# A peer-expert stage on one core: the residual on GpSimd, differences of p with six products, and the ones of c in bfloat16 from SBUF

## The chip, the core and the metric

The kernel runs on one core of a Trainium2 chip. The metric is device time in microseconds (us), the median over the runs shown; a profile is one execution with the hardware profiler on. The core has five engines with a queue of instructions each: TensorE (PE; its weight loads are shown as PEld), VectorE (DVE), ScalarE (ACT), GpSimd (POOL) and SyncE (SP), which here issues the transfers. An engine works through its queue in order and waits at an instruction until what it reads is written and what it writes over has been read.

## The reference

The inputs are 16 sequences of 512 tokens with 128 features. An attention with a window (16 heads, a token sees the 128 tokens before and after it) is added to x; then comes a layer with 1024 small experts, whose result is added too:

```python
s, i = jax.lax.top_k(sim, k)                      # per head: 8 best of 32 keys, twice
all_scores = (sx[..., :, None] + sy[..., None, :]).reshape(b, n, h, k * k)
all_idx = (ix[..., :, None] * nk + iy[..., None, :]).reshape(b, n, h, k * k)
scores, pk = jax.lax.top_k(all_scores, k)         # the 8 best of 64 sums
idx = jnp.take_along_axis(all_idx, pk, axis=-1)
w_down = key_in[idx]
w_up = key_out[idx]
o = jnp.einsum('bnd,bnhkd->bnhk', inputs, w_down)
o = jax.nn.gelu(o, approximate=False) * jax.nn.softmax(scores, axis=-1)
return jnp.einsum('bnhk,bnhkd->bnd', o, w_up)
```

So each token picks 8 heads times 8 = 64 experts (by number), with a share each.

## The kernel before

Two stages follow each other. The first is the attention, with the normalisations; the change leaves it alone. It ends with x after attention in SBUF (`xs[b]`) and its normalised transpose in DRAM.

The second stage, the experts, gathers nothing: all 1024 experts are computed for every token, and the picked ones are weighted. The number of an expert is written as p * 16 + c, with 64 values of p (`NP`) and 16 of c (`NC`). It works through 64 tiles of 128 tokens, i = 0 to 63; tile i is quarter t = i % 4 of sequence b = i // 4. For one tile:

1. DVE finds the best keys (`best_keys`, `where_keys`), the best sums and their places (`best_sums`, `where_sums`), POOL and DVE make the expert numbers from them (`pick_words` on POOL: two `word` instructions; then `numbers` on DVE, whose first instruction, `x_ps<-word,x_ps`, needs the second word). Below, t and "tile" mean this loop.
2. `turn`: ACT casts the numbers to bfloat16 (`num_bf`), PE transposes them into a PSUM bank (`turned`, in the profile `x_ps`) so that the 64 picks lie on the partitions, and 64 tokens of each half of the tile along the row. `turned[:, 0]` holds p times 16 and `turned[:, 1]` holds c. ACT copies the p part to `p_bf`.
3. Indicators ("ones") are made: of c on DVE (`ones_of_c`, tile `mine`: is c of this pick equal to 0..15?), multiplied on POOL with the pick's share (`weights_at_c`, four instructions, tile `cols`); of p for one half of the tokens on DVE (`ones_of_p`, two `row` instructions), for the other half through differences: PE puts p minus each number 0..63 into PSUM (`offs_of_p`, `off_ps`: four banks, two products each), ACT squares them (`off_p`) and takes Relu(1 - square) (`other_ones_of_p`, `row`).
4. `weigh`: for each token PE multiplies the indicators of p with the weighted indicators of c, which gives the tile's weight for every expert (`w_ps`); 128 small matmuls a tile in two halves, `m` = 0 and 1. ACT copies them out (`take_weights`, tile `g`), POOL multiplies by the gelu of the experts' inner products (`weigh_experts`, `g<-g,gel`).
5. PE multiplies with the experts' output rows (`up`, for an earlier sequence, a quarter at a time), and `finish` transposes a finished sequence (`o_ps`); `store` adds the residual and sends it off.

Beside it run the inner products of the next sequence (`down` on PE, `dn_ps`; `gelu` on ACT) and the scores of the tile after next (`score`, `take_scores`).

Every engine's order is written out by hand in the loop: whatever goes through `pe`, `dve`, `act`, `pool` keeps program order. What sets the order around the change, in one turn of the loop for tile i: `best_sums(i)`, the weights of half 0 of tile i-1, `where_sums`, `pick_words`, `numbers(i)`, `weigh(i-1, 1)` and half a quarter of `up` (`seconds`), `turn(i)`, `share_of(i)` and `sums_of_keys(i+1)` on POOL, the weights of half 1 of tile i-1, `where_keys(i+1)`, `offs_of_p(i)`, `turn_shares(i)` (`s_ps`), the ones of c and p, the other half of `seconds`, `down`, `score(i+2)` (`sim_ps`), the gelu, at t = 1 `scale` (`xb`) for the next sequence, and then, at t = 1, `finish` and `store` of sequence b-2, and `weigh(i, 0)`.

The PSUM pool `ps_x` has three buffers, used in turn by `off_ps`, `dn_ps`, `sim_ps` and `o_ps`. Lines 168, 172 and 615 of the profile are helpers that record operations, so one line stands for many; the tiles' names tell them apart. L330 is the normalisation on DVE, L368 and L369 are memsets in the attention stage: L369 writes one of every 32 numbers of a row (`va[:, :, :, DK : DK + 1]`).

Of the kernel before, what the change touches and what calls it, by code (L numbers as in the profile page):

```python
# [10 lines left out]
F32 = mybir.dt.float32  # L11
BF16 = mybir.dt.bfloat16
# [4 lines left out]
ALU = mybir.AluOpType  # L17
# [3 lines left out]
P = 128  # L21
# [6 lines left out]
def bc(ap, axis, n):  # L28

    ap = ap.unsqueeze(axis)  # L30
    shape = list(ap.shape)
    shape[axis] = n
    return ap.to_broadcast(shape)
# [10 lines left out]
def kernel(  # L44
# [13 lines left out]
    nc = tc.nc  # L58
    B, T, D = x.shape
    NH = 16  # L60
    DK = D // NH
    NQ = T // P
# [8 lines left out]
    const = ctx.enter_context(tc.tile_pool(name="const", bufs=1))  # L71
# [8 lines left out]
    xs = []  # L80
    for b in range(B):
        t = keep.tile([P, NQ, D], F32, name=f"x_{b}")
# [8 lines left out]
    NP, NC = P // 2, NE // (P // 2)  # L91
# [3 lines left out]
    ident = const.tile([P, P], F32, name="ident")  # L95
    make_identity(nc, ident)
    ident_bf = const.tile([P, P], BF16, name="ident_bf")
# [18 lines left out]
    def counted(shape, pattern, dtype, name, base=0):  # L116

        t_i = const.tile([P] + shape, I32, name=f"{name}_i")
        nc.gpsimd.iota(t_i, pattern=pattern, base=base, channel_multiplier=0)
        if dtype == I32:  # L120
            return t_i
        t = const.tile([P] + shape, dtype, name=name)
        nc.vector.tensor_copy(t, t_i)
        return t
# [2 lines left out]

    nums_p = counted([NP], [[NC, NP]], F32, "nums_p")
    nums_c = counted([NC], [[1, NC]], F32, "nums_c")
    less_nums = const.tile([P, NP], BF16, name="less_nums")  # L130
    nc.vector.tensor_scalar_mul(less_nums, nums_p, -1.0)

# [17 lines left out]
    out_v = out.rearrange("b (t p) d -> b p t d", p=P)  # L150


    with ExitStack() as at:
# [385 lines left out]
        for s in range(-2 * NG * NQ, (NU + 1) * NQ):  # L539
            n, u = divmod(s, NQ)  # L540
            b, g = divmod(n, NG)
# [53 lines left out]
    b2 = ctx.enter_context(tc.tile_pool(name="b2", bufs=2))  # L595
# [3 lines left out]
    ps_x = ctx.enter_context(tc.tile_pool(name="ps_x", bufs=3, space=PSUM))  # L599
    ps_t = ctx.enter_context(tc.tile_pool(name="ps_t", bufs=1, space=PSUM))  # L600
    HK = H * TOPK
    HT, QT = P // 2, P // 4
    NM = QT // 2
    HM = NM // 2
    halves = [slice(v * HT, v * HT + HT) for v in range(2)]
# [11 lines left out]
    pe, dve, act, pool = (InOrder(e) for e in (nc.tensor, nc.vector, nc.scalar, nc.gpsimd))  # L617
# [9 lines left out]
    xbs, downs, gels, gs, ups, outs_T = {}, {}, {}, {}, {}, {}  # L627
    sims, tops, cands, idxs, bytes_of, steps_of = {}, {}, {}, {}, {}, {}
    bests, ws, shares, places, shifts, words, nums, turned = {}, {}, {}, {}, {}, {}, {}, {}
    mines, rows, weights = {}, {}, {}  # L630
    p_bfs, wTs, offs = {}, {}, {}

    def scale(b):
        xb = b2.tile([P, T], F32, tag="xb", name=f"xb_{b}")
# [67 lines left out]
    def best_sums(j):  # L702
        best = b2.tile([P, H, TOPK], F32, tag="best", name=f"best_{j}")
        for h in range(H):
            dve.max(best[:, h], cands[j][:, h].rearrange("p a b -> p (a b)"))
        bests[j] = best
# [55 lines left out]
    def turn(j):  # L762

        num = b2.tile([P, 3, HK], BF16, tag="num_bf", name=f"num_bf_{j}")
        act.copy(num, nums.pop(j))
        for i, (to, what) in enumerate(((0, num[:, 0]), (0, num[:, 1]), (1, num[:, 2]))):
            for v in range(2):
                pe.matmul(
                    turned[j][halves[v], to], lhsT=what, rhs=ident_bf[:, halves[v]],
                    start=i == 0, stop=i != 0, skip_group_check=True,  # L770
                )
        p_bfs[j] = b2.tile([P, HT], BF16, tag="p_bf", name=f"p_bf_{j}")
        act.copy(p_bfs[j], turned[j][:, 0])

    def turn_shares(j):
        share = shares.pop(j).rearrange("p h k -> p (h k)")
# [9 lines left out]
    def take_shares(j):  # L786
        wT = b2.tile([P, HT], F32, tag="wT", name=f"wT_{j}")
        act.copy(wT, wTs[j])
        wTs[j] = wT

    def some(t, m, rows_of=slice(0, P)):

        return t.rearrange("p (v m n) -> p m v n", v=2, m=2)[rows_of, m]

    def ones_of_c(j):
        mine = b2.tile([P, 2, 2, NM, NC], BF16, tag="mine", name=f"mine_{j}")
        dve.tensor_tensor(
            mine.rearrange("p v m n c -> p (v m n) c"), bc(turned[j][:, 1], 2, NC),
            bc(nums_c, 1, HT), ALU.is_equal,
        )  # L800
        mines[j] = mine

    def weights_at_c(j, m):
        for s in range(2):
# [5 lines left out]
    def ones_of_p(j, m):  # L810
# [3 lines left out]
            ALU.is_equal,  # L814
        )

    def offs_of_p(j):

        for m in range(2):
            for n in range(0, NM, HM):  # L820
                off_ps = ps_x.tile([P, HM, NP], F32, tag="x", name=f"off_ps_{j}_{m}_{n}")
                for start, rhs in (
                    (True, bc(some(p_bfs[j], m)[:, 1, n : n + HM], 2, NP)),
                    (False, bc(less_nums, 1, HM)),
                ):
                    pe.matmul(off_ps, lhsT=ident_bf, rhs=rhs, start=start, stop=not start)
                off_p = b2.tile([P, HM, NP], BF16, tag="off_p", name=f"off_p_{j}_{m}_{n}", bufs=4)
                act.activation(off_p, off_ps, AF.Square)
                offs[j, m, n] = off_p
# [21 lines left out]
    def take_weights(j, m):  # L851
        b, t = divmod(j, NQ)
        if t == m == 0:
            gs[b] = b2.tile([P, NC, NQ, 2, QT], F32, tag="g", name=f"g_{b}")
        g = gs[b][:, :, t, :, m * NM : m * NM + NM]
        act.copy(g, weights.pop((j, m)).rearrange("p n (s c) -> p c s n", s=2))

    def weigh_experts(j, m):

        b, t = divmod(j, NQ)  # L860
        g = gs[b][:, :, t, :, m * NM : m * NM + NM]
        pool.tensor_tensor(g, g, gels[b][:, :, t, :, m * NM : m * NM + NM], ALU.mult)
# [17 lines left out]
    def finish(b):  # L880

        oT = outs_T.pop(b)
        o_ps = ps_x.tile([P, NQ, D], F32, tag="x", name=f"o_ps_{b}")
        for t in range(NQ):
            pe.transpose(
                o_ps[:, t], oT[:, 2 * t : 2 * t + 2].rearrange("d s v n -> d (s v n)"), ident
            )
        outs_T[b] = o_ps

    def store(b):  # L890
        o_sb = b2.tile([P, NQ, D], F32, tag="o_sb", name=f"o_sb_{b}")
        dve.tensor_add(o_sb, outs_T.pop(b), xs[b])
        nc.sync.dma_start(out_v[b], o_sb)


# [3 lines left out]
    NB = B * NQ  # L899

    def seconds(i, place):

        b, t = divmod(i, NQ)
        if b + 1 == B and t in (1, 2):
            up(b - 1, range(8 * t - 8 + 4 * place, 8 * t - 4 + 4 * place))
        elif i + 1 == NB:
            if place:
                up(b, range(NC), slice(0, NQ // 2))
        else:
            of, quarter = (b - 1, t - 1) if t else (b - 2, NQ - 1)  # L910
            if of >= 0:
                c = 4 * quarter + 2 * place
                up(of, range(c, c + 2))
# [19 lines left out]
    for i in range(NB):  # L933
        b, t = divmod(i, NQ)
        before, behind = i > 0, i + 1 < NB
        best_sums(i)
        less_greatest(i)
        if before:
            take_weights(i - 1, 0)
        step_of_words(i)  # L940
        where_sums(i)
        pick_words(i)
        if before:
            weigh_experts(i - 1, 0)
        tops_of = best_keys(i + 1) if behind else iter(())
        next(tops_of, None)
        numbers(i)
        if before:
            weigh(i - 1, 1)
        seconds(i, 0)  # L950
        turn(i)
        for _ in tops_of:
            pass
        share_of(i)
        if behind:
            sums_of_keys(i + 1)
        if before:
            take_weights(i - 1, 1)
            weigh_experts(i - 1, 1)
        if behind:  # L960
            where_keys(i + 1)
        offs_of_p(i)
        turn_shares(i)
        take_shares(i)
        if behind:
            pack_keys(i + 1)
        for m in range(2):
            rows[i, m] = b2.tile([P, 2, NM, NP], F32, tag="row", name=f"row_{i}_{m}")
        ones_of_c(i)
        weights_at_c(i, 0)  # L970
        ones_of_p(i, 0)
        ones_of_p(i, 1)
        weights_at_c(i, 1)
        other_ones_of_p(i, 0)
        other_ones_of_p(i, 1)
        seconds(i, 1)
        if b + 1 < B:
            down(b + 1, 2 * t)
            down(b + 1, 2 * t + 1)
        if i + 2 < NB:  # L980
            score(i + 2)
            take_scores(i + 2)
        if b + 1 < B:
            gelu(b + 1, 2 * t)
            gelu(b + 1, 2 * t + 1)
        if t == 1:
            if b + 1 < B:
                scale(b + 1)
            if b + 2 < B:
                load(b + 2)  # L990
        ready = b - 2 if t == 1 else b - 1 if i + 1 == NB else -1
        if ready >= 0:
            finish(ready)
            store(ready)
        weigh(i, 0)
    take_weights(NB - 1, 0)
    weigh_experts(NB - 1, 0)
# [42 lines left out]
```

## Time and profile before

| what | us |
|---|---|
| three runs: median (lowest, highest) | 1604.19 (1594.6, 1605.45) |
| the profiled execution, its own time | 1607.73 |
| its span, first to last instruction | 1606.0 |
| first and last `best` of the experts' stage, start | 771.7, 1574.8 |

| engine | busy us in the span | share |
|---|---|---|
| PE | 1438.7 | 90% |
| DVE | 1359.5 | 85% |
| ACT | 1208.8 | 75% |
| POOL | 1078.4 | 67% |

The mean granted TensorE clock was 0.976 of full speed. The table's shares are over both stages, and the stages differ: a question about the experts has to be put to the rows of that stage.

A row of the timeline is read as: start and length in us, engine, line, operation, what is written <- what is read with sizes, how many merged, and in brackets how long the engine had stood idle before it and whose end released it. In a row of the instruction groups the numbers behind the bar are busy us, mean ns of one, and idle us before them.

### The profile page before, as it was taken

How to read it: one execution, taken by the hardware profiler on the slowest of the kernel's cores; microseconds unless marked ns; L12 is line 12 of the kernel's file. 1: busy time of each engine (PE TensorE's matmuls, PEld its weight loads, DVE VectorE, ACT ScalarE, POOL GpSimd, SP SyncE). 2: the span in 40 equal slices, each digit the busy share in tenths (PEclk: the TensorE clock that was granted, in tenths of full speed). 3: DMA queues.
4: the chain of work that ended last, by engine and by line, in shares of the span. 5: the costliest groups of instructions: out<-in, count | busy, mean ns of one | idle time of the engine just before them, and what ended most of it. 6: DMA issues, size and time to landing. Idle time of an engine off the chain costs nothing.

```text
span 1606.0 us, 49399 instructions
## 1 busy us (share of the span) xinstructions
PE 1438.7 (90%) x16880; PEld 844.4 (53%) x16880; DVE 1359.5 (85%) x8012; ACT 1208.8 (75%) x2579; POOL 1078.4 (67%) x1692
## 2 busy tenths in 40 slices
PE   4899999999999999986789999999999999999998
PEld 1344454444444444433456666666666666666666
DVE  6788778778878888885799999999999999999994
ACT  1477667667767777676698888888898888988863
POOL 7466666666667666545477777777777777777774
PEclk9899999999999999999799999999999999999998
DMA  6233322222223223221000000000000000000000
GB/s 180 66 103 95 95 76 81 79 70 80 71 71 94 86 81 96 82 61 53 9 9 10 9 15 9 15 16 9 15 9 15 16 9 16 9 16 9 9 9 14
DMA packets 53579, 75.00 MB, mean 47 GB/s; under 512 B 5840, under 2 KB 39888, under 8 KB 53200
## 3 DMA queue, kind: packets, MB, share of 16 engines
q1 hardware_dynamic: 52496, 71.59, 15.2%
q8 instruction: 133, 2.18, 0.6%
q14 instruction: 118, 0.97, 0.2%
q10 hardware_dynamic: 832, 0.26, 0.1%
HBM read 49.28 MB, written 20.97 MB: 44 GB/s over the span
## 4 chain that ended last, share of the span: by engine, by line
PE 36%; DVE 35%; ACT 10%; DMA 9%; POOL 6%; issue 3%; SPq 2%; DVEq 0%; POOLq 0%; ACTq 0%
PE o_ps L168 7%; PE s_ps L168 7%; DVE idx L615 7%; DVE row L615 6%; PE e_ps L168 5%; DMA qst<-qv 5%; DVE place L615 4%; DVE top L615 4%; DMA qst<-mT 4%; DVE best L615 3%; DVE mine L615 3%; PE off_ps L615 3%; PE dn_ps L615 3%; ACT L615 2%; DVE masked L415 2%
## 5 line engine op out<-in xcount | busy, mean ns | idle before, releaser
L415 DVE CUSTOM_DVE_ANT_0 masked<-s_ps,band 128x384 bf16<-128x384 f32 (+1 forms) x1024 | 498.3, 487 | 142.6 <-PE s_ps L168 40.4
L457 ACT ACTIVATE pT<-e_ps 128x384 f32<-128x384 f32 (+1 forms) x1024 | 390.6, 436 | 173.1 <-PE e_ps L168 165.2
L172 POOL TENSOR_SCALAR_AFFINE_SELECT pT<-pT 128x512 f32<-128x512 f32 x384 | 238.8, 638 | 238.9 <-ACT pT L457 238.8
L168 PE MATMUL s_ps<-kst,qst 128*128 128x384 bf16 (+1 forms) x1024 | 314.1, 308 | 45.9 <-DVE mx L415 14.9
L615 POOL TENSOR_TENSOR cols<-mine,wT 64x512 f32<-64x512 bf16 x256 | 269.8, 1054 | 51.8 <-DVE mine L615 29.1
L615 PEld LDWEIGHTS w_ps<-cols,row 128*64 128x64 f32 x8192 | 250.2, 139 | 48.4 <-POOL cols L615 42.8
L615 PE MATMUL w_ps<-cols,row 128*64 128x32 f32 x8192 | 259.4, 224 | 6.8 <-POOL cols L615 6.8
L168 PE MATMUL e_ps<-qst,kst 128*128 128x384 bf16 (+1 forms) x1024 | 226.8, 303 | 11.5 <-DMA qst<-mT 7.3
L615 POOL TENSOR_TENSOR g<-g,gel 128x512 f32<-128x512 f32 x128 | 163.6, 1278 | 87.9 <-ACT g L615 87.9
L168 PEld LDWEIGHTS <-qst 128*128 128x128 bf16 x1024 | 100.4, 98 | 217.6 <-issue 159.0
L168 PE MATMUL o_ps<-pT,vaug 128*32 128x384 f32 (+1 forms) x2048 | 192.8, 448 | 0.4 <-POOL pT L172 0.4
L615 DVE FIND_INDEX8 idx<-top,sim 128x8 uint32<-128x32 f32 x1024 | 166.2, 184 | 0.0
L615 ACT ACTIVATE row<-off_p,one 128x512 f32<-128x512 bf16 x256 | 165.7, 748 | 0.0
L615 ACT ACT_TABLE_LOAD x122 | 156.5, 1283 | 2.1
L615 DVE TENSOR_TENSOR row<-x_ps,nums_p 128x1024 f32<-128x1024 f32 x128 | 150.0, 1212 | 0.0
L615 PE MATMUL up_ps<-g,key_out_sb 64*128 64x256 f32 (+2 forms) x1152 | 148.1, 384 | 0.0
L615 ACT ACTIVATE off_p<-off_ps 128x512 bf16<-128x512 f32 x256 | 133.4, 601 | 19.4 <-PE off_ps L615 19.2
L615 PE MATMUL dn_ps<-xt,key_inT 128*64 128x256 f32 x1024 | 128.8, 396 | 0.0
L168 PEld LDWEIGHTS <-kst 128*128 128x128 bf16 x1024 | 98.1, 99 | 53.0 <-issue 19.2
L615 PE MATMUL off_ps<-p_bf,ident_bf 128*128 128x512 bf16 x256 | 99.1, 387 | 19.5 <-ACT p_bf L615 19.5
L615 DVE MAX8 top<-sim 128x8 f32<-128x32 f32 x1024 | 106.7, 177 | 5.5 <-ACT sim L615 5.5
L615 PEld LDWEIGHTS up_ps<-g,key_out_sb 64*128 64x128 f32 x1152 | 95.3, 189 | 12.4
(143 smaller groups left out, 2326.0 us busy)
## 6 DMA issues: line engine op xcount, KB each, us to landing
qst<-qv SPq DMA_DIRECT2D x192, 96.0 KB
kst<-kv SPq DMA_DIRECT2D x192, 96.0 KB
qv<-qp SPq DMA_DIRECT2D x16, 384.0 KB
kv<-kp SPq DMA_DIRECT2D x16, 384.0 KB
x<-in_L_attn_x_dram SPq DMA_DIRECT2D x16, 256.0 KB
xT<-xiT SPq DMA_DIRECT2D x16, 256.0 KB
xt<-xT SPq DMA_DIRECT2D x16, 256.0 KB
out_dram<-o_sb SPq DMA_DIRECT2D x16, 256.0 KB
```

Of the source, the lines that this page charges most:

```text
L168: tc.keep_in_program_order(nc.tensor.matmul(*args, **kw))
L172: tc.keep_in_program_order(getattr(nc.gpsimd, op)(*args, **kw))
L415: nc.vector.tensor_tensor_reduce(masked[:, 0:w], s, band.rearrange("p u k -> p (u k)")[:, from_u : from_u + w], 1.0, LOWEST, ALU.add, ALU. ...
L457: nc.scalar.activation(pT[:, h, 0:w], e_ps[:, 0:w], AF.Exp)
L615: return lambda *args, **kw: tc.keep_in_program_order(op(*args, **kw))
```

## The change

Three things are changed in the experts' stage, and two constants are added for them.

- The residual: at t = 1 ACT copies the transposed result from PSUM (`take_outs`), and in the next tile, t = 2, POOL adds x and the store is issued (`add_and_store`), between `take_weights(i - 1, 1)` and `weigh_experts(i - 1, 1)`. The last two sequences still use `store` on DVE.
- The differences of p: minus the numbers is put into two PSUM banks by two products before `turn` (`less_of_p`); then p of half m = 0 is added to them, ACT squares, and the difference between p of half 1 and p of half 0 is added to the same banks, and ACT squares again. For that the transposition uses `steps_bf` in place of the identity for p, so that the last 16 columns are differences. `p_bf` becomes 96 columns wide: the second half of p, and c.
- The ones of c: `mine` is compared from `p_bf` and a table `each_c` of all 16 values in 64 columns, both bfloat16 in SBUF; `mine` lies as (c, tokens) and is handed to `weights_at_c`, which is unchanged, as a view with c innermost.

```diff
+    steps_bf = const.tile([P, 2, P // 2], BF16, name="steps_bf")
+    nc.vector.tensor_copy(steps_bf.rearrange("p s n -> p (s n)"), ident)
+    for s in range(2):
+        nc.vector.tensor_sub(
+            steps_bf[:, s, 48:64], ident[:, 64 * s + 48 : 64 * s + 64],
+            ident[:, 64 * s + 32 : 64 * s + 48],
+        )
+    each_c = const.tile([P, NC, P // 2], BF16, name="each_c")
+    nc.vector.tensor_copy(each_c, bc(nums_c, 2, P // 2))
...
-                    turned[j][halves[v], to], lhsT=what, rhs=ident_bf[:, halves[v]],
+                    turned[j][halves[v], to], lhsT=what,
+                    rhs=ident_bf[:, halves[v]] if to else steps_bf[:, v],
...
-        p_bfs[j] = b2.tile([P, HT], BF16, tag="p_bf", name=f"p_bf_{j}")
-        act.copy(p_bfs[j], turned[j][:, 0])
+        p_bfs[j] = b2.tile([P, QT + HT], BF16, tag="p_bf", name=f"p_bf_{j}")
+        act.copy(p_bfs[j], turned[j].rearrange("p i n -> p (i n)")[:, QT : QT + QT + HT])
...
-        mine = b2.tile([P, 2, 2, NM, NC], BF16, tag="mine", name=f"mine_{j}")
-        dve.tensor_tensor(
-            mine.rearrange("p v m n c -> p (v m n) c"), bc(turned[j][:, 1], 2, NC),
-            bc(nums_c, 1, HT), ALU.is_equal,
-        )
-        mines[j] = mine
+        mine = b2.tile([P, NC, HT], BF16, tag="mine", name=f"mine_{j}")
+        dve.tensor_tensor(mine, bc(p_bfs[j][:, QT : QT + HT], 1, NC), each_c, ALU.is_equal)
+        mines[j] = mine.rearrange("p c (v m n) -> p v m n c", v=2, m=2)
...
+    def less_of_p(j):
+        diffs[j] = [ps_x.tile([P, HM, NP], F32, tag="x", name=f"off_ps_{j}_{i}") for i in range(2)]
+        for off_ps in diffs[j]:
+            pe.matmul(
+                off_ps, lhsT=ident_bf, rhs=bc(less_nums, 1, HM), start=True, stop=False,
+                skip_group_check=True,
+            )
...
-                off_ps = ps_x.tile([P, HM, NP], F32, tag="x", name=f"off_ps_{j}_{m}_{n}")
-                for start, rhs in (
-                    (True, bc(some(p_bfs[j], m)[:, 1, n : n + HM], 2, NP)),
-                    (False, bc(less_nums, 1, HM)),
-                ):
-                    pe.matmul(off_ps, lhsT=ident_bf, rhs=rhs, start=start, stop=not start)
+                off_ps = diffs[j][n // HM]
+                tokens = bc(p_bfs[j][:, m * NM + n : m * NM + n + HM], 2, NP)
+                pe.matmul(
+                    off_ps, lhsT=ident_bf, rhs=tokens, start=False, stop=True,
+                    skip_group_check=True,
+                )
...
+    def take_outs(b):
+        o_sb = b2.tile([P, NQ, D], F32, tag="o_sb", name=f"o_sb_{b}")
+        act.copy(o_sb, outs_T[b])
+        outs_T[b] = o_sb
+
+    def add_and_store(b):
+        o_sb = outs_T.pop(b)
+        pool.tensor_tensor(o_sb, o_sb, xs[b], ALU.add)
+        nc.sync.dma_start(out_v[b], o_sb)
...
         seconds(i, 0)
+        less_of_p(i)
         turn(i)
...
             take_weights(i - 1, 1)
+            if t == 2 and b >= 2:
+                add_and_store(b - 2)
             weigh_experts(i - 1, 1)
...
-        ready = b - 2 if t == 1 else b - 1 if i + 1 == NB else -1
-        if ready >= 0:
-            finish(ready)
-            store(ready)
+        if t == 1 and b >= 2:
+            finish(b - 2)
+            take_outs(b - 2)
+        if i + 1 == NB:
+            finish(b - 1)
+            store(b - 1)
         weigh(i, 0)
```

## The prediction

> **What bounds the kernel now.** I read the busy time by stretch first. The experts' stage runs from about 770 us to the end, 64 token tiles, and in its middle each 100 us looks like this (span, then busy time of PE, its weight loads, DVE, ACT, POOL; clock; DMA share; GB/s):
>
> ```profile
> 1100.00:1200.00 100.00, 91.99 (x1445) 62.27 (x1442) 94.12 (x675) 87.35 (x163) 73.58 (x96) 1.00 0.05 13
> ```
>
> Three engines are near full, POOL has a quarter free, the clock is full. So shares decide nothing, and I followed one group of four tiles (one sequence b, t = 0 to 3) in the timeline, engine by engine. ACT, columns start, length, instruction, idle before it:
>
> ```profile
> 1205.15 0.59 ACT L615 COPY sim<-sim_ps 128x512 f32<-128x512 f32 x1 [0.73 <-PE sim_ps L615]
> ...
> 1212.02 0.35 ACT L615 CAST num_bf<-num 128x192 bf16<-128x192 uint32 x1 [1.14 <-DVE num L615]
> ...
> 1231.38 0.59 ACT L615 COPY sim<-sim_ps 128x512 f32<-128x512 f32 x1 [0.73 <-PE sim_ps L615]
> ...
> 1236.31 0.35 ACT L615 CAST num_bf<-num 128x192 bf16<-128x192 uint32 x1
> ...
> 1243.53 0.59 ACT L615 COPY sim<-sim_ps 128x512 f32<-128x512 f32 x1 [0.26 <-PE sim_ps L615]
> ```
>
> PE and DVE in the same stretch:
>
> ```profile
> 1236.71 0.28 PE L615 MATMUL x_ps<-ident_bf,num_bf 128*64 128x64 bf16 x6 [0.35 <-ACT num_bf L615]
> ...
> 1239.16 0.34 PE L615 MATMUL s_ps<-ident,share 128*64 128x64 f32 x4
> ...
> 1242.37 1.13 PE L615 MATMUL sim_ps<-wsim,xb 128*128 128x512 f32 x2
> ```
>
> ```profile
> 1206.49 0.69 DVE L615 TENSOR_TENSOR o_sb<-o_ps,x 128x512 f32<-128x512 f32 x1 [2.39 <-PE o_ps L615]
> ...
> 1234.91 0.29 DVE L615 TENSOR_TENSOR x_ps<-word,x_ps 128x128 uint32<-128x128 uint32 x1
> ...
> 1239.29 1.20 DVE L615 TENSOR_TENSOR mine<-x_ps,nums_c 128x1024 bf16<-128x1024 f32 x1
> ```
>
> The reader is to see a ring through ACT and PE: ACT goes from sim to num_bf in 1236.31 + 0.35 - 1231.38 = 5.28 us, PE from x_ps to the end of sim_ps in 1243.50 - 1236.71 = 6.79, and with the hand-overs that is 12.15 us, sim to sim. DVE alone would need 11.87 a tile (it starts 1218.93, 1230.80, 1242.67) and catches up only because it is held once in four tiles: 2.39 us for o_ps plus 0.69 for the residual. The group takes 50.5 us (o_sb 1206.49 to 1257.01): three tiles near 12.15 and one of 14.
>
> POOL has its own ring, which is nearly as long:
>
> ```profile
> 1233.27 0.29 POOL L615 TENSOR_TENSOR w<-best 128x64 f32<-128x64 f32 x1
> ...
> 1234.45 0.43 POOL L615 TENSOR_TENSOR word<-word,packed 128x128 int32<-128x128 int32 x1
> 1236.49 1.28 POOL L615 TENSOR_TENSOR g<-g,gel 128x512 f32<-128x512 f32 x1 [1.61 <-ACT g L615]
> ...
> 1239.00 1.28 POOL L615 TENSOR_TENSOR g<-g,gel 128x512 f32<-128x512 f32 x1
> 1240.64 4.42 POOL L615 TENSOR_TENSOR cols<-mine,wT 64x512 f32<-64x512 bf16 x4 [0.36 <-DVE mine L615]
> ```
>
> Call T the end of the second word (1234.88). DVE's x_ps (numbers) starts 0.03 later, mine at T+4.41, the four cols at T+5.76 to T+10.18, and w, step, word, word need 1.41 (w's start 0.08 after cols): T' = T+11.7. So POOL's idle time is only inside the ring's DVE part; any lateness of cols over about 0.5 us becomes the tile's period.
>
> **The change, part by part.**
>
> *Residual.* DVE loses 0.69 + 2.39 us once in four tiles. But behind it ACT is next: sim at 1205.15, table load, two gel, xb 0.81, table load, w, g: num_bf could have started at 1210.88 (1212.02 less its idle 1.14). ACT now also copies o_ps (like the g copy, 0.59), so num_bf starts near 1211.45: gain 0.55 us of the 3.1 seen on DVE. POOL gets 128x512 f32 add once in four tiles, 1.28 by the g row, ahead of the second g and of cols. The store's DMA only moves half a tile later; nothing on SP waits for it.
>
> *Six products.* PE drops two of eight off_ps products at 0.215 (start to start). But two move ahead of x_ps, and PE waits there only 0.35 (and not at all in tile t = 3), so up to 0.4 comes on the ring. The third and fourth now write a bank that ACT's Square still reads: p_bf product, Square (0.60), product, Square. From 1237.30 (off_ps's first start) on: first Square 1237.74 (after ACT's g copy) to 1238.34, third product 1238.38, second Square to 1238.83, fourth product 1238.87, next matmul 1239.09 against 1239.16. So nothing is gained on PE; p_bf's 96 instead of 64 columns costs 0.03. Net 0 to +0.4 us a tile.
>
> *Ones of c on DVE.* mine is 1.20 us for 1024 outputs, or 1.12 start to start. No two-input bf16 operation from SBUF is in this trace, so: at worst 1.20 as now; by the Trainium skill (VectorE: DVE Perf Modes, the perf-mode tier table) tensor_tensor in dense bf16 from SBUF goes at twice the rate, so 512 of its 1024 cycles, 0.53 us at 0.96 GHz, go: 0.67. I take 0.67. On the ACT-PE ring it is worth nothing; on POOL's ring it brings cols forward 0.53.
>
> *Ones of c on POOL.* The new mine lies as (c, token); cols still reads c innermost, so each of its 512 elements now comes from 128 bytes further (64 bf16) instead of the next address. No POOL read of this kind is in the trace. The nearest rows are a 128-byte-stride write and a 16-byte-stride read of 16 elements:
>
> ```profile
> L615 POOL TENSOR_TENSOR step<-packed 128x16 int32<-128x16 int32 x64 | 15.0, 234 | 0.0
> ...
> L368 POOL MEMSET vaug<- 128x2048 f32 x3 | 5.4, 1815 | 0.0
> L615 POOL MEMSET cols<- 128x1024 f32 x2 | 1.8, 952 | 6.5 <-DVE bn_a L586 6.5
> L369 POOL MEMSET vaug<- 128x64 f32 x3 | 0.6, 209 | 0.0
> ```
>
> Dense memsets cost 863/1024 = 0.84 ns an element and about 90 fixed, so 64 dense elements would be 145; the strided ones took 209: +1.0 ns each. For step, the rows of 64 and 512 elements (w 294, cand 1066) give 1.72 ns an element and 184 fixed, 212 for 16; it took 234 with two strided inputs: +0.7 ns per strided element. So cols (1054) becomes 1.41 to 1.57. The Trainium skill (GPSIMD Engine Reference, Performance pitfalls for Q7 kernels) says that a read step over 8 bytes takes about 2.9 cycles an element instead of 1.9: +0.83 ns at its 1.2 GHz, 1.48. Bounds: below, +0, if the strided read hides behind the second operand (a gain has no reason); above, 1.7. I take 1.47, 0.42 a piece and 1.7 us a tile.
>
> *The shared port.* mine had one SBUF input, now two. No row has two long SBUF inputs on DVE; the nearest are normalisations from SBUF in the attention stage:
>
> ```profile
> 188.20 0.64 POOL L172 TENSOR_SCALAR_AFFINE_SELECT pT<-pT 128x512 f32<-128x512 f32 x1 [2.17 <-ACT pT L457]
> 188.22 0.69 DVE L330 TENSOR_SCALAR xn<-x,mva,rsa 128x128 f32<-128x128 f32 x1
> ...
> 189.31 0.34 DVE L330 TENSOR_SCALAR xn<-x,mva,rsa 128x128 f32<-128x128 f32 x1
> ```
>
> The same operation takes 0.34 alone and 0.69 beside POOL's select, ending with it; experts' row, with PSUM beside it, doesn't stretch (1.21 each). The skill (SBUF — State Buffer, Who interferes with whom) says that a DVE instruction with two SBUF inputs and a GpSimd one that reads SBUF hold a port by turns. Without it mine starts at T+4.41; with it, when the second g ends, if later.
>
> *The sum.* Normal tile: cols start T+4.41+0.67+0.15 = T+5.23, end 4.42 + 4 x 0.42 = 6.1 later, +1.49 for w to word: period 12.83. PE's x_ps then waits for weigh 1 after cols, up and two less_nums products (T+2.1), its sim ends T+8.9, ACT's next g is ready at T+14.0, so POOL's first g starts 14.0 - P into the next tile and its second ends 3.8 after that; with the port rule mine starts there: P = (14.0 - P + 3.8) + 0.82 + 6.1 + 1.49, P = 13.1. I use 13.0. In tile t = 2 ACT comes 1.4 later (xb, the new copy): first g at T+2.4, share, cand, the residual, second g to T+7.45, then cols: 7.5 + 6.1 + 1.5 = 15.1. Group: 3 x 13.0 + 15.1 = 54.1 against 50.5, +3.6. Thirteen such groups give 47; the first two (no residual yet) 3 each by 4 x 13.0 against 4 x 12.15; the last, without scores to prepare, 0 to 2. About +53 us; the setup copies of the new constants lie under the first loads. The profiled execution is 1607.7 (span 1606.0 and 1.7 around it), so 1661; the median 1604.2 stands 3.5 lower: 1657.
>
> **The rivals.**
>
> *B: the strided read costs nothing.* Then cols end at T+9.7, POOL's ring is shorter than 12.15, and the ACT-PE ring stays: t = 2 gains 0.55 to 1 and gives part of it back, since its cols wait for the residual (g ends T+6 or so, PE's second weigh about 1 us late in t = 3), and the six products cost 0 to 0.4 a tile. Group 50 to 51: 1596 to 1614. For it: cols' 2.06 ns an element may be POOL's program and not its reads; it decides below 1.3 us a piece, as D shows. Against: both strided rows above.
>
> *C: DVE is the bound after all* (it heads the chain of waits with 35%). Then 3.1 us a group and 0.53 a tile go, 5.2 of 50.5, down to 1521 at the most; the ACT-PE ring, 12.15 untouched, stops it at 48.6, 16 x 1.9 = 30 us: 1574. Against: in three tiles of four DVE's period is 11.87 and PE's 12.15.
>
> *D: the stride is dearer.* At 1.8 us a cols piece POOL's ring is 14.2, group about 59: 1735. The price from which POOL decides at all is 1.3 us a piece (ring 12.2 with the earlier mine).
>
> That the change doesn't do what it says, DVE staying at 1.20 for mine, would add 0.53 to POOL's ring: 1685 in case A.
>
> **How the numbers follow.** Case A (POOL's ring) 0.66, B 0.20, C 0.08, D 0.06. One per cent, about what a measurement of this kernel tells from no change, is 16 us: A and D are slower (A touches +16 only with cols under 1.35), most of B is within it, C faster. Faster 0.08, same 0.17, slower 0.75. The likeliest, A with cols at 1.47, gives 1655; cols from 1.35 to 1.6 make it 1625 to 1695. The range reaches down into B: 1605 to 1692.
>
> **What would show it.** In the changed profile: cols mean 1.4 to 1.55 us; mine near 0.67, longer where POOL's g runs; POOL above 85% busy, its first g with under 1 us of idle time; DVE idle before x_ps, released by POOL's word; no o_sb wait of 2.4; tile starts 13 apart and 15 once in four. The prediction is wrong if cols stay at 1.05, or if the tiles keep 12.15 with longer cols.

## The result, and the profile after

| | us |
|---|---|
| changed kernel, median of 4 runs (lowest, highest) | 1665.55 (1664.23, 1670.56) |
| kernel before, 4 runs | 1599.81 (1594.60, 1605.45) |
| ratio, with 95% interval | 1.0396 [1.0363, 1.0429] |
| span of the profiled execution, before and after | 1606.0 and 1662.5 |

The change makes the kernel 4% slower. The time is in the experts' stage: the first `best` starts at 771.9 us (before 771.7), the last at 1632.3 (before 1574.8).

First the instruction groups of POOL and DVE that matter, before (L615) and after (L626), with busy us, mean ns of one, and idle us before them:

```profile
L615 POOL TENSOR_TENSOR cols<-mine,wT 64x512 f32<-64x512 bf16 x256 | 269.8, 1054 | 51.8 <-DVE mine L615 29.1 <-ACT wT L615 4.7 <-ACT packed L615 2.7
...
L615 DVE TENSOR_TENSOR x_ps<-word,x_ps 128x128 uint32<-128x128 uint32 x64 | 18.9, 296 | 1.0 <-POOL word L615 1.0
```

```profile
L626 POOL TENSOR_TENSOR cols<-mine,wT 64x512 f32<-64x512 bf16 x256 | 343.9, 1343 | 54.4 <-ACT wT L626 27.6 <-DVE mine L626 11.8 <-ACT packed L626 1.0
...
L626 POOL TENSOR_TENSOR o_sb<-o_sb,x 128x512 f32<-128x512 f32 x14 | 23.8, 1698 | 0.0
```

```profile
L626 DVE TENSOR_TENSOR mine<-p_bf,each_c 128x1024 bf16<-128x1024 bf16 x64 | 61.6, 962 | 8.4 <-ACT p_bf L626 8.4
L626 DVE TENSOR_SCALAR upper<-place 128x64 uint32<-128x64 uint32 x128 | 58.6, 498 | 2.2
...
L626 DVE TENSOR_TENSOR x_ps<-word,x_ps 128x128 uint32<-128x128 uint32 x64 | 18.9, 296 | 67.5 <-POOL word L626 67.5
```

`cols` went from 1054 to 1343 ns: the strided read costs 289 ns for 512 elements, 0.56 each. `mine` fell to 962 on the mean, but its shortest is 672 and its longest 1672 in the view of that tile, which is not one speed. And DVE now stands idle 67.5 us in front of `numbers`, released by POOL's second word; before, that was 1.0 us. So POOL's ring, from one second word to the next, has become the period. Here it is in POOL's timeline (start, length, idle before):

```profile
1224.46 0.42 POOL L626 TENSOR_TENSOR word<-word,packed 128x128 int32<-128x128 int32 x1
1225.87 1.27 POOL L626 TENSOR_TENSOR g<-g,gel 128x512 f32<-128x512 f32 x1 [0.99 <-ACT g L626]
...
1228.37 1.28 POOL L626 TENSOR_TENSOR g<-g,gel 128x512 f32<-128x512 f32 x1
1230.35 5.57 POOL L626 TENSOR_TENSOR cols<-mine,wT 64x512 f32<-64x512 bf16 x4 [0.70 <-ACT wT L626]
...
1237.03 0.43 POOL L626 TENSOR_TENSOR word<-word,packed 128x128 int32<-128x128 int32 x1
1240.11 1.27 POOL L626 TENSOR_TENSOR g<-g,gel 128x512 f32<-128x512 f32 x1 [2.66 <-ACT g L626]
...
1242.62 1.73 POOL L626 TENSOR_TENSOR o_sb<-o_sb,x 128x512 f32<-128x512 f32 x1
1244.32 1.27 POOL L626 TENSOR_TENSOR g<-g,gel 128x512 f32<-128x512 f32 x1
1245.56 5.56 POOL L626 TENSOR_TENSOR cols<-mine,wT 64x512 f32<-64x512 bf16 x4
...
1252.23 0.42 POOL L626 TENSOR_TENSOR word<-word,packed 128x128 int32<-128x128 int32 x1
```

From the second word of a tile to that of the next ("word to word") it is 12.57 us in the first of these tiles (t = 1) and 15.20 in the second (t = 2). The DVE rows of the same stretch:

```profile
1209.23 1.21 DVE L626 TENSOR_SCALAR upper<-place 128x64 uint32<-128x64 uint32 x2
...
1216.23 1.38 DVE L626 TENSOR_TENSOR mine<-p_bf,each_c 128x1024 bf16<-128x1024 bf16 x1
...
1224.91 0.30 DVE L626 TENSOR_TENSOR x_ps<-word,x_ps 128x128 uint32<-128x128 uint32 x1 [0.27 <-POOL word L626]
...
1242.51 0.70 DVE L626 TENSOR_TENSOR mine<-p_bf,each_c 128x1024 bf16<-128x1024 bf16 x1
```

`mine` took 0.70 where it started at 1242.51, just ahead of POOL's add (1242.62), and the add then took 1.73 instead of 1.27. At 1216.23 POOL was in its second g, which ended at 1217.07, and `mine` took 1.38: it ended 0.54 us after that g. In these two places, whoever came first held the other.

Over four tiles, word to word, groups at full clock compare so: before 11.86 + 11.87 + 11.87 + 14.92 = 50.5 (the prediction's three tiles of 12.15 and one of 14 are the same group, counted from sim to sim); after 15.14 + 12.59 + 13.07 + 12.57 = 53.4. But some groups are longer: one tile t = 3 lasts 15.58 instead of 12.59. The reason is seen on PE (first fence: the two halves of `weigh` in the group before, then in this one) and in its clock (second fence: span, then busy time of PE, weight loads, DVE, ACT and POOL, then the clock, third from the end, DMA share and GB/s; the last two rows are from the group before):

```profile
1194.94 2.06 PE L626 MATMUL w_ps<-cols,row 128*64 128x32 f32 x64 [1.02 <-POOL cols L626]
1197.75 2.06 PE L626 MATMUL w_ps<-cols,row 128*64 128x32 f32 x64 [0.75 <-POOL cols L626]
...
1248.36 2.06 PE L626 MATMUL w_ps<-cols,row 128*64 128x32 f32 x64 [1.04 <-POOL cols L626]
1251.18 3.63 PE L626 MATMUL w_ps<-cols,row 128*64 128x32 f32 x64 [0.76 <-POOL cols L626]
1254.74 2.08 PE L626 MATMUL up_ps<-g,key_out_sb 64*128 64x256 f32 x8
```

```profile
1247.57:1250.98 3.41, 2.06 (x64) 1.95 (x64) 1.96 (x17) 3.36 (x5) 3.28 (x3) 1.00 0.02 5
1250.98:1254.40 3.42, 3.22 (x61) 3.23 (x62) 1.65 (x13) 1.74 (x4) 2.67 (x6) 0.50 0.00 0
1254.40:1257.81 3.41, 3.41 (x22) 1.69 (x22) 2.74 (x33) 0.00 (x0) 1.31 (x2) 0.50 0.03 5
1192.96:1196.37 3.41, 2.39 (x52) 1.56 (x52) 3.15 (x30) 2.46 (x5) 3.20 (x4) 1.00 0.00 0
1196.37:1199.78 3.41, 2.66 (x88) 2.51 (x84) 0.49 (x3) 2.58 (x5) 3.17 (x6) 1.00 0.02 5
```

PE waits twice for the late cols of tile t = 2, and the granted clock then drops to half for 6.8 us (the two rows with 0.50); the same 64 matmuls take 3.63 us instead of 2.06. Between 850 and 1540 us such a drop happens five times after and never before.

Why not in every group, when the waits recur in each? The five drops start at 977.92, 1141.76, 1250.98, 1360.21 and 1524.05 us, which lie 48, 32, 32 and 48 times 3.413 us apart: the clock changes only on a grid with that step, and so it does in the experts' stage of every run here. The groups shift against the grid. In the group with the drop, the two waits lie for the most part in one step, and PE is busy for 2.06 of its 3.41 us; in the group before, equal waits fall into two steps, with 2.39 and 2.66. Of the 13 tiles t = 3 in this stretch, five begin (second word) 0.80 to 1.80 us after a grid point, and these are the five with a drop; the other eight begin elsewhere.

### The profile page after: what moved, and what is told of

It is laid out like the page before. It is cut to its first block, busy times and chain, and to the rows that moved or that the text cites. A ratio compares the mean times of both kernels' runs of the same rounds, so it can differ in the third digit from the quotient of the medians.

```text
span 1662.5 us, 48961 instructions
## 1 busy us (share of the span) xinstructions
PE 1448.2 (87%) x16752; PEld 837.6 (50%) x16752; DVE 1378.2 (83%) x8002; ACT 1220.7 (73%) x2593; POOL 1172.4 (71%) x1706
## 4 chain that ended last, share of the span: by engine, by line
PE 36%; DVE 23%; POOL 18%; ACT 9%; DMA 7%; issue 5%; SPq 1%; DVEq 0%; POOLq 0%; ACTq 0%
POOL cols L626 9%; PE o_ps L179 7%; PE s_ps L179 7%; DVE idx L626 6%; PE e_ps L179 5%; DMA qst<-qv 5%; DVE row L626 4%; PE w_ps L626 3%; DVE masked L426 3%; PE up_ps L626 3%; DMA qst<-mT 3%; DVE mine L626 2%; ACT L626 2%; PE dn_ps L626 2%; ACT pT L468 2%
## 5 line engine op out<-in xcount | busy, mean ns | idle before, releaser
L626 POOL TENSOR_TENSOR cols<-mine,wT 64x512 f32<-64x512 bf16 x256 | 343.9, 1343 | 54.4 <-ACT wT L626 27.6
L626 PE MATMUL w_ps<-cols,row 128*64 128x32 f32 x8192 | 273.2, 228 | 47.4 <-POOL cols L626 42.6
L626 PEld LDWEIGHTS w_ps<-cols,row 128*64 128x64 f32 x8192 | 260.3, 143 | 93.5 <-POOL cols L626 91.1
L626 POOL TENSOR_TENSOR g<-g,gel 128x512 f32<-128x512 f32 x128 | 163.8, 1280 | 96.2 <-ACT g L626 96.2
L626 DVE FIND_INDEX8 idx<-top,sim 128x8 uint32<-128x32 f32 x1024 | 166.2, 185 | 0.0
L626 ACT ACTIVATE row<-off_p,one 128x512 f32<-128x512 bf16 x256 | 164.1, 721 | 0.0
L626 PE MATMUL up_ps<-g,key_out_sb 64*128 64x256 f32 (+2 forms) x1152 | 152.6, 393 | 0.0
L626 DVE TENSOR_TENSOR row<-x_ps,nums_p 128x1024 f32<-128x1024 f32 x128 | 149.9, 1210 | 0.0
L626 ACT ACTIVATE off_p<-off_ps 128x512 bf16<-128x512 f32 x256 | 137.4, 595 | 1.4 <-PE off_ps L626 1.4
L626 PE MATMUL off_ps<-p_bf,ident_bf 128*128 128x512 bf16 x256 | 87.9, 385 | 57.6 <-ACT off_p L626 29.5
L626 PE MATMUL dn_ps<-xt,key_inT 128*64 128x256 f32 x1024 | 128.1, 394 | 0.0
L626 DVE MAX8 top<-sim 128x8 f32<-128x32 f32 x1024 | 106.8, 177 | 4.6 <-ACT sim L626 4.6
L626 PEld LDWEIGHTS up_ps<-g,key_out_sb 64*128 64x128 f32 x1152 | 97.4, 193 | 13.1
```

Of the source, the lines that this page charges most:

```text
L626: return lambda *args, **kw: tc.keep_in_program_order(op(*args, **kw))
```

## The experiments

Each ratio is to the kernel before, run beside it. Besides the time, the table has four tiles that follow each other (word to word, at full clock, in the middle of the stage); the rows do not all begin at the same t.

| run | median us | ratio [95%] | four tiles, us | sum |
|---|---|---|---|---|
| ones of c alone | 1635.62 | 1.0206 [1.0185, 1.0226] | 12.67 14.40 12.38 12.44 | 51.9 |
| strided layout only | 1659.26 | 1.0357 [1.0335, 1.0379] | 12.91 14.37 12.88 12.88 | 53.0 |
| two SBUF inputs only | 1616.62 | 1.0063 [1.0039, 1.0087] | 14.24 11.90 12.44 12.16 | 50.7 |
| residual alone | 1592.16 | 0.9938 [0.9912, 0.9963] | 14.33 11.87 11.86 11.86 | 49.9 |
| six products alone | 1610.02 | 1.0058 [1.0034, 1.0081] | 15.31 11.86 11.87 11.87 | 50.9 |
| changed, old ones of c | 1600.09 | 0.9993 [0.9976, 1.0011] | 12.18 14.44 11.87 12.04 | 50.5 |
| ones of c and residual | 1669.73 | 1.0421 [1.0376, 1.0466] | 12.40 12.71 12.41 14.81 | 52.3 |
| ones of c and six | 1643.24 | 1.0267 [1.0221, 1.0313] | 13.05 14.94 12.40 12.57 | 53.0 |
| changed, add earlier | 1632.25 | 1.0191 [1.0148, 1.0234] | 12.62 13.93 12.62 13.04 | 52.2 |
| late store | 1584.90 | 0.9888 [0.9850, 0.9926] | 13.46 11.86 11.87 12.09 | 49.3 |
| late store, scale | 1579.43 | 0.9863 [0.9828, 0.9897] | 11.86 11.87 11.86 13.08 | 48.7 |
| late store, scale, gelu first | 1573.63 | 0.9830 [0.9798, 0.9861] | 11.86 11.86 11.86 12.76 | 48.3 |

**Each part alone.** Ones of c alone is the kernel before with the new `mine`, `each_c` and the 96-column `p_bf`:

> The kernel before with the new ones of c alone (p_bf 96 columns wide, comparison from SBUF in bfloat16 with c outermost); residual and products of p as before. Theory A (POOL's ring through the strided read of cols decides): cols 1.34 us a piece as in the changed kernel, POOL's ring 4.41 + 0.67 + 0.15 + 5.6 + 1.49 = 12.3 us without a wait for the port and about 12.6 with it, so some 1 us a group of four: 1610 to 1635. Theory B (the residual on POOL and ACT costs the time) and theory C (the six products do): 1600 or less, since DVE becomes shorter and nothing else changes.

1635.6, just above the range. `cols` takes 1345 ns here, and the tiles go from 11.87 to 12.4 to 12.7. This part alone costs 2.1%. Not all of it is in the groups: the first eight tiles, from second word to second word, take 117.7 us instead of 104.7, and the clock drops five times there (792 to 857 us), against two drops in this stretch before (810 and 834).

Residual alone (`take_outs`, `add_and_store`):

> The kernel before with the residual on ACT and POOL alone. Theory A: o_sb's wait on DVE goes, ACT's copy costs 0.6 on the ACT-PE ring, the add (1.70 on POOL) delays cols in tile t = 2: 1592 to 1606, no change that can be told. Theory B: slower, 1620 or more. If DVE were the bound: 1560.

1592.2: a small gain. DVE loses its 3.1 us a group, and the group becomes 0.6 us shorter, which is what the ACT-PE ring allowed. In this run the add takes 1.27 us; no `mine` with two SBUF inputs stands beside it. Six products alone:

> The kernel before with the differences of p by six products alone (p_bf 32 columns wide). Theory A: PE has the two less_nums products ahead of x_ps (0.54 us in the changed kernel's rows) where it waited 0.35 us in two tiles of four, nothing in one and 1.06 in one, and the four others take as long as the eight did: +1 us a group, 1608 to 1622. Theory C: most of the loss is here, 1640 or more. If fewer products relieve PE: 1575 to 1590.

1610.0, +0.4 us a group. PE's row for the two early products is 0.60 us; from x_ps to s_ps it takes 2.42 us (1201.96 to 1204.38), where before it took 2.45 (1236.71 to 1239.16): fewer products, no time saved. Four groups here also have a short drop of the clock, of 3.4 us, and are about 1.2 us longer; 14 x 0.4 and 4 x 1.2 make up the 10 us.

**What of the ones of c costs.** The layout without the second SBUF input:

```diff
-        mine = b2.tile([P, 2, 2, NM, NC], BF16, tag="mine", name=f"mine_{j}")
-        dve.tensor_tensor(
-            mine.rearrange("p v m n c -> p (v m n) c"), bc(turned[j][:, 1], 2, NC),
-            bc(nums_c, 1, HT), ALU.is_equal,
-        )
...
+        mine = b2.tile([P, NC, HT], BF16, tag="mine", name=f"mine_{j}")
+        dve.tensor_tensor(mine, bc(turned[j][:, 1], 1, NC), each_c, ALU.is_equal)
...
```

> The kernel before, with mine laid out with c outermost but still compared from PSUM: one SBUF input and no double rate, so no port to wait for; only the read of cols is strided. Theory A: cols 1.34, mine 1.20, ring 4.41 + 1.20 + 0.15 + 5.6 + 1.49 = 12.85 against 12.15, +0.7 a tile: 1630 to 1650. Theory B and C: 1600. A theory D (the shared port is what costs, not the stride): 1600 to 1610 here.

1659.3, above what was expected. Its groups of instructions (first fence) and, for one input more and no stride (`bc(p_bfs[j][:, QT : QT + HT], 2, NC)` compared with a bfloat16 copy of `nums_c`, c innermost), those of the other run (second fence; in the view by tile the numbers are shortest, median and longest ns):

```profile
L617 POOL TENSOR_TENSOR cols<-mine,wT 64x512 f32<-64x512 bf16 x256 | 344.9, 1347 | 96.5 <-DVE mine L617 59.3 <-ACT wT L617 21.7 <-DVE row L617 2.2
...
L617 DVE TENSOR_TENSOR mine<-x_ps,each_c x64: 1203/1212/1225, 781.8 to 1632.4; 128x1024 bf16<-128x1024 f32 x64
```

```profile
L617 POOL TENSOR_TENSOR cols<-mine,wT 64x512 f32<-64x512 bf16 x256 | 269.4, 1052 | 93.3 <-DVE mine L617 67.4 <-ACT wT L617 12.5
...
L617 DVE TENSOR_TENSOR mine<-p_bf,nums_c_bf x64: 1211/1522/2249, 788.6 to 1594.5; 128x1024 bf16<-128x1024 bf16 x64
```

> The kernel before, with the comparison from two SBUF inputs in bfloat16, but laid out with c innermost, so that cols reads densely (no double rate, since one input repeats each number). cols 1.05. If the port is held by turns, mine starts only when POOL's second g ends: its longest are above 2 us, and the tile goes to about 12.4: 1612 to 1628. If not, mine stays at 1.2 and the time at 1600.

The two runs take the change's part apart. With the stride, `mine` is steady at 1.2 and `cols` takes 1.35: tiles of 12.9, +3.6%. With two SBUF inputs, `cols` is steady at 1.05 and `mine` swings from 1.21 to 2.25: +0.6%. So the stride is the cost; the wait between DVE and POOL is real but small here; and the double rate of `mine` (672 ns at its shortest) gives back a part, 1.1 us a group (51.9 against 53.0). The rest of the step from 3.6% to 2.1% is the clock: with the stride alone it drops three times between 1050 and 1500 us, and those tiles last 17.24 instead of 14.37, 8.6 us in all. These are tiles t = 1, and there is no add on POOL in that run, so the drop does not need the new residual.

**Undoing it in the changed kernel** (only `ones_of_c` as before):

> The changed kernel with mine compared and laid out as before (from PSUM, c innermost). Theory A: cols back to 1.05, POOL's ring is shorter than 12.15 again, the time returns to the kernel before plus what the six products cost: 1600 to 1622. Theories B and C: it stays near 1665.

1600.1, even with the kernel before: the residual's 0.6% gain and the six products' 0.6% loss cancel. But then the ones of c cost 4.0% in the changed kernel and 2.1% alone. Pairs show with what they interact (if two parts only added up, their ratios would multiply):

> The changed kernel without the six products (differences of p as before; ones of c and residual as changed). The ones of c alone gave a group of 51.9 us against 50.5, all three changes 53.4. If the add of 1.70 us on POOL ahead of cols is what turns the residual from a gain into a loss, a tile t = 2 near 15 us appears here and the group is 52.5 to 53: 1640 to 1655. If the two only add up (1.0206 x 0.9938), 1622 to 1630.

> The changed kernel with the residual on DVE as before. If the six products only add what they cost alone (0.6%), 1640 to 1650, with a group near 52.3; if they cost more beside a longer ring of POOL, because PE has its two less_nums products behind the late weigh, tiles grow by up to 0.5 each: 1650 to 1660.

With the residual: 1669.7, above the range and the whole loss; the two ratios alone would give 1.0206 x 0.9938 = 1.014. Its group at full clock is only 0.4 us longer than that of the ones of c alone (52.3 against 51.9; 14 x 0.4 = 6 us of the 34 us between the two). The rest is the clock: it drops to half seven times between 860 and 1540 us here and never in the run of the ones of c alone; in five of the seven, the tile t = 3 lasts 16.35 where others last 12.40. With the six products instead, one drop and a group of 53.0. Beside the longer ring they cost 1.1 us a group, against 0.4 alone: PE comes to x_ps without a wait in three tiles of four in both runs, so that the two early products, 0.53 us there, lie on its path. In the total this does not show, 1.0267 against 1.0206 x 1.0058 = 1.0265, since the first eight tiles are 6.5 us shorter than with the ones of c alone. So it is the residual that interacts, and mostly through the clock.

**The place of the add.**

```diff
         pick_words(i)
+        if t == 2 and b >= 2:
+            add_and_store(b - 2)
...
             take_weights(i - 1, 1)
-            if t == 2 and b >= 2:
-                add_and_store(b - 2)
             weigh_experts(i - 1, 1)
```

> The changed kernel with the add on POOL in the same tile t = 2 but behind pick_words, ahead of the first product with gelu, where POOL's rows show 2.66 us of idle time in that tile. If the add costs because of its place on POOL's ring, tile t = 2 falls from 15.1 to about 13.6 and the time by 14 x 1.5 = 21, more if the clock no longer drops: 1630 to 1648. If ACT's copy is what delays tile t = 2, no change: 1660 or more.

POOL's timeline of a tile t = 2 of that run:

```profile
1219.36 0.43 POOL L626 TENSOR_TENSOR word<-word,packed 128x128 int32<-128x128 int32 x1
1220.37 1.27 POOL L626 TENSOR_TENSOR o_sb<-o_sb,x 128x512 f32<-128x512 f32 x1 [0.59 <-ACT o_sb L626]
1222.42 1.27 POOL L626 TENSOR_TENSOR g<-g,gel 128x512 f32<-128x512 f32 x1 [0.78 <-ACT g L626]
1224.92 1.73 POOL L626 TENSOR_TENSOR g<-g,gel 128x512 f32<-128x512 f32 x1
1226.61 5.58 POOL L626 TENSOR_TENSOR cols<-mine,wT 64x512 f32<-64x512 bf16 x4
...
1233.29 0.43 POOL L626 TENSOR_TENSOR word<-word,packed 128x128 int32<-128x128 int32 x1
```

The add lies in time in which POOL waited for ACT anyway, the tile is 13.93 instead of 15.1 to 15.2, cols start 7.25 us after the start of the second word instead of 8.53, and the clock is at full speed from 850 to 1540 us. 1632.3 is 33 us less: 17 by the group (14 x (53.4 - 52.2)), about 15 by the five drops at 3.0 each.

**Is the ACT-PE ring what bounded the kernel before?** If so, it should get faster by taking things off that ring, with no work removed. First `finish` moves ahead of `turn` in tile t = 2 and `store`, still on DVE, behind `share_of`; then `scale` moves ahead of `take_scores`; then the gelu too:

```diff
+        if t == 2 and b >= 2:
+            finish(b - 2)
         turn(i)
...
         share_of(i)
+        if t == 2 and b >= 2:
+            store(b - 2)
...
         if i + 2 < NB:
             score(i + 2)
-            take_scores(i + 2)
         if b + 1 < B:
             gelu(b + 1, 2 * t)
             gelu(b + 1, 2 * t + 1)
+        if i + 2 < NB:
+            take_scores(i + 2)
...
```

> The kernel before, with finish moved from the end of tile t = 1 to ahead of turn in tile t = 2 and the residual still on DVE, behind share_of of that tile. By the ACT-PE ring: num_bf of tile t = 2 comes at 1210.9 instead of 1212.0 (DVE no longer held 3.1 us), 1.1 us a group less up to 0.6 for the transposition ahead of x_ps: 1585 to 1600. If DVE is the bound: 1565.

> The same, and scale (xb, 0.81 us on ACT) moved ahead of take_scores in tile t = 1, where ACT waits 0.73 us for PE's sim. By the ACT-PE ring xb leaves the ring too: group 4 x 12.15 + 0.6 = 49.2 against 50.5: 1572 to 1590. If DVE is the bound, no difference to the run with the late store alone.

> The kernel with the late store and the earlier scale, and ACT's two gelu moved ahead of take_scores (their dn_ps are ready before sim_ps, and ACT stands idle for 0.73 us there). On the ACT-PE ring only the copy of sim, a table load, w, g and num_bf stay behind sim_ps: up to 0.7 us less a tile until DVE's 11.87 limits it, group 4 x 11.87 + 0.7 = 48.2 against 48.7: 1565 to 1577. If the ring is not what bounds that kernel: 1579 as without it.

1584.9 lies at the lower edge of its range, 0.1 us outside; 1579.4 and 1573.6 lie in theirs. The first is far from the 1565 expected if DVE were the bound. In the last, ACT's row of num_bf shows who leads:

```profile
1208.24 1.28 ACT L615 ACT_TABLE_LOAD   x1
1209.54 1.09 ACT L615 ACTIVATE gel<-dn_ps 128x512 f32<-128x512 f32 x2
1210.51 0.59 ACT L615 COPY sim<-sim_ps 128x512 f32<-128x512 f32 x1
...
1213.46 0.35 ACT L615 CAST num_bf<-num 128x192 bf16<-128x192 uint32 x1 [0.32 <-DVE num L615]
```

ACT no longer waits for sim, and num_bf waits for DVE: three tiles in four are 11.86, DVE's own sum. This version is faster than both kernels. In this state time taken from DVE should count, which no run tried; in the state before, 3.1 us of it were worth 0.6.

## Why the prediction was right, and where it was not

- *The bound before* (ACT-PE ring of 12.15, DVE not the bound): shown by the residual alone (3.1 us off DVE, 0.6 us off the group) and by the last three runs.
- *cols at 1.47*: the mechanism was right, the size too large. 1.343: 0.56 ns a strided element. Of the two rows that bounded it, the 16-byte read (0.7) was nearer than the strided write (1.0). The +0.83 taken from the Trainium skill (GPSIMD Engine Reference, Performance pitfalls for Q7 kernels) was too much for this two-input operation; why, no run shows. The price from which POOL decides does not follow from the prediction's own terms: 5.23 + 4 x 1.3 + 1.49 is 11.9, not 12.2, and with the measured 1.343 it is 12.09, still under 12.15.
- *mine at 0.67*: 672 ns is the shortest in the trace. *The port by turns*: shown in both directions (mine 1.38 beside g; the add 1.73 beside mine), as the Trainium skill says of two such instructions (SBUF — State Buffer, Who interferes with whom). What it adds to a tile was about as reckoned: in the tile from 1224.88 (word's end), mine came 4.41 later as predicted, and took 0.91.
- *Normal tiles at 13.0*: 12.59, 13.07 and 12.57. The fuller sum, in which mine waits for POOL's second g and that for ACT, holds: with 1.343 in place of 1.47 it gives 12.74, the mean of the three. *Tile t = 2 at 15.1*: 15.14; here luck helped. Its term of 1.28 for the add missed that `mine` would hold it (1.73), and the shorter cols made up for that; it also has no term for mine behind the second g, which its own rule on the port asks for, and mine happened to get in just ahead of the add. The group: 53.4 against 54.1.
- *Six products at 0 to 0.4 a tile*: 0.1 alone, 0.3 beside the longer ring.
- *What failed*: the sum took the PE clock as granted in full, and its +53 us consisted of longer tiles alone. Longer tiles give about 14 x 2.9 = 41 us; the five drops add 15. That +53 came near the span's +56.5 is luck in part: tiles put 12 us too long against a clock put at nothing. The signs named to look for also failed in two places: POOL is 79% busy in 1100 to 1200 us, not above 85%, and its first g still waits 1.0 to 2.7 us for ACT in three tiles of four. A ring can set the period with idle time inside it.
- *The rivals*: B (a free strided read) falls with the 1343 ns, C (DVE the bound) with the residual alone, D with the size.

Not shown: that the waits, and not something else of that tile, make the clock drop. No run filled PE's gap with other matmuls; it rests on the pattern: none once the add is moved, and in the three runs that lose most to the clock between 850 and 1540 us (changed, ones of c and residual, strided layout only) drops in all 15 tiles (t = 3, in the last run t = 1) that begin 0.73 to 1.80 us after a grid point and in none of the 23 others. PE's busy share alone does not decide: the kernel before has steps with 2.05 of 3.41 us busy (957.46 to 960.87) and no drop.

## What to carry to other kernels

Making an operand cheaper to produce can make it dearer to read: the layout that gave DVE twice the rate put a stride of 128 bytes into four POOL instructions on the longest ring, and 64 savings of up to 0.5 us cost 256 times 0.29. When three engines are all near 90%, follow one item around the loop (who waits for whom until the same instruction comes again) and price an edit by the ring it lies on: 3.1 us off DVE was worth 0.6, and moving two gelu into a wait gained 5.8 us (1579.4 to 1573.6), where removing two matmuls a tile lost 10. A small operation moved to an engine with spare time belongs where that engine waits, not ahead of what others wait for.

## What the runs showed of the hardware

- TensorE's granted clock changes on a grid of 3.413 us. It halves for 6.8 us after waits of only 1.04 and 0.76 us that fall into one step of it (PE busy for 2.06 of 3.41 us), and not after equal waits that fall into two; a tile with such a drop of two or three steps costs 2.7 to 4.0 us more. The Trainium skill (TensorE: Matmul & The Clock Gate, The HAM clock gate) names an idle window of about 3.4 us for it; here no single wait was as long.
- DVE's `upper`, a short operation with a single input in SBUF, is held by POOL too: 0.29 us for two before, 1.21 at 1209.23 with `cols` beside it. In the changed kernel 48 of its 128 are longer than 0.3 us, and each of them ends 0.05 us after a piece of `cols`.
- A 128-byte read step costs POOL 0.56 ns an element in a two-input operation, in every run with that layout (1342 to 1347 ns, against 1052 to 1055 where it reads densely).
